# Another order for the first loads of a fused attention and feed-forward kernel: two tiles of x, projection weights, two tiles, then eleven weight blocks

## Chip, cores and metric

The kernel runs on one core of a Trainium2 chip. The metric is the device time of one execution in microseconds; lower is better.

## What is computed

The input x has shape (4, 512, 512): a batch of four, 512 tokens, 512 features. Cut to what matters:

```python
xn = layernorm(x)                                  # over the features, no weights
q, k, v = split(xn @ w_qkv)                        # 16 heads of 32
q, k = rope(rmsnorm(q, q_gamma)), rope(rmsnorm(k, k_gamma))
s = softmax(causal(q @ k.T / sqrt(32))) @ v @ w_out
W = lambda wq, scale: (wq - 128.0) * scale[:, None]  # int32 weights, 1408 hidden
g = silu((silu(xn @ W_gate.T) * (xn @ W_up.T)) @ W_down.T)
return x + s * g
```

All arrays are float32 but the three quantised weights, which are int32.

## The kernel before

The work is cut into 16 units, one for each batch `b` of four and each group `g` of four heads. A unit is a *hidden window* (`hidden_window`: the gate and up products of two or three blocks of 128 hidden columns, in `chunks[g]`) and an *attention window* (`attention_window`: scores, softmax and values of four token tiles `s[0]` to `s[3]`, with the down products `contract` and the projection and rotation of the next unit between them). Nothing plans this at run time: the pools are under a manual schedule, so each engine executes its instructions in the order in which the program writes them. What an engine waits for holds up all that is written after it on that engine. This applies to SyncE (SP) and its DMA queue too.

Ahead of the first unit stands `prologue`. It normalises the four tiles of batch 0, projects them for group 0, and starts the pipeline of the weights. Its parts, with the lines of the profile:

- `load_x` (L122) loads one tile of 128 tokens on SP. `Norm.stats` (L315, L316) takes mean and variance on VectorE, `Norm.roots` (L301, L302) the inverse root on GpSimd, `Norm.apply` (L323) scales the tile in place on VectorE, `Norm.turn` (L331, L334, L335) transposes it on TensorE and copies it on ScalarE twice, as `xnT` and as its rounded `xh`; `Norm.low` (L339) forms the rest `xl` on GpSimd.
- `Projection.product` (L353) multiplies one tile by the q, k and v columns of one group: four matmuls of fp32. `Projection.rotate` applies the norm of q and k and the rotary table: a square and a copy of v on ScalarE (L368, L369), three products and a sum on VectorE (L381, L384, L388), then four GpSimd instructions (L389, L301, L302, L391). `Projection.turn` (L401) transposes q and k into `qT` and `kT` at the third stop of the first hidden window.
- `prepare_table` (L193, L196) folds `q_gamma` and `k_gamma` (tile `gam`) into the rotary table `tab`.
- An int32 weight block goes through three stages. `load_weights` (L236) loads a block of 256 KB into a free room; `turn_weights` casts it on ScalarE (L245) and transposes it by DMA on SP (L247); `finish_weights` (L254) subtracts 128 on VectorE and writes the final weights. Blocks come in a fixed order: gate and up of hidden block 0 and 1 (g0, u0, g1, u1), four down blocks (d0 to d3), then g2, u2, g3, u3, g4 and so on. There are eleven rooms at the start, so that at most eleven blocks can be loaded before one is finished.
- `load_wqkv` (L147) loads the projection weights of group 0 ahead of the prologue in four pieces of 192 KB, and those of the other three groups at its end in four pieces of 576 KB. `sdown` is a broadcast row of 256 KB (L803).

Within the windows of batch 0, `weights()` keeps this pipeline going. At each call it finishes up to two blocks that were turned at least two calls ago, loads two more, and turns two that were loaded at least one call ago:

```python
for _ in range(n):
    if turning and now[0] - turning[0][0] >= 2:
        finish_weights()
load_weights(n)
for _ in range(n):
    if loaded and now[0] - loaded[0][0] >= 1:
        turn_weights()
```

The first hidden window calls it twice, after each of its two hidden blocks. So on ScalarE the casts of g2 and u2 are written between the SiLU of the first hidden block (L532) and that of the second, ahead of the copy of `qT` (L114); the casts of g3 and u3 are written ahead of the first exponentials (L447). On TensorE the order there is: gate and up of block 0 (L521), gate of block 1, the transposes of q and k (L401), up of block 1, the first scores (L419), the first down products (L549), scores, down products, the transposes of the first probabilities (L463), and the projection of the next unit.

Of the kernel before, what the change touches and what calls it, by code (L numbers as in the profile page):

```python
# [21 lines left out]
P = 128  # L22
# [3 lines left out]
NT = N // P  # L26
# [25 lines left out]
def interleaved(  # L52
# [27 lines left out]
    nc = tc.nc  # L80
# [19 lines left out]
    def work(name):  # L100
        return wk.tile([P, N], F32, tag="wk", name=name)
# [18 lines left out]
    def load_x(b, t):  # L120
        xt = xp.tile([P, D], F32, tag="x", name=f"x_{b}_{t}")
        nc.sync.dma_start(xt, xf[ts(b * NT + t, P), :])  # L122
        x_tiles[b, t] = xt
# [7 lines left out]

    ident = const.tile([P, P], F32, name="ident")
    make_identity(nc, ident)
    for t in range(NT):
        load_x(0, t)

    gam = work("gam")[:, 0 : 4 * HD].rearrange("p (a c d) -> p a c d", a=2, c=2)
    for i, g in enumerate((q_gamma, k_gamma)):
        nc.scalar.dma_start(gam[:, i, 0, :], g.partition_broadcast(P))
    tab = const.tile([P, NT, 2, 2, HD], F32, name="tab")  # L140
    nc.scalar.dma_start(tab, rope.rearrange("(t p) a c d -> p t a c d", p=P))

    wqkv = const.tile([P, NC, 3, NC, P], F32, name="wqkv")

    def load_wqkv(groups):
        for c in range(NC):
            nc.sync.dma_start(  # L147
                wqkv[:, c, :, groups, :],
                w_qkv[ts(c, P), :].rearrange("p (i g d) -> p i g d", i=3, g=NC)[:, :, groups, :],
            )  # L150

    load_wqkv(slice(0, 1))


    mask = const.tile([P, N], F32, name="mask")
# [18 lines left out]
    def load_scales():  # L174
        srow = work("srow")
        at = 0
        for s in (s_gate, s_up):
            n = s.shape[0] // P
            nc.sync.dma_start(srow[at : at + n, 0:P], s.rearrange("(c p) -> c p", p=P))
            at += n  # L180
        return srow, at
# [3 lines left out]
    def prepare_scales(srow, at):  # L185
        tp = bank_t("sps")
        nc.tensor.transpose(tp[:, 0:at], srow[0:at, 0:P], ident[0:at, 0:at])
        nc.vector.tensor_copy(scales, tp[:, 0:at])

    def prepare_table():  # L190

        for lo, hi in ((0, half), (half, 0)):
            nc.vector.tensor_copy(gam[:, :, 1, lo : lo + half], gam[:, :, 0, hi : hi + half])  # L193
        tab_f = tab.rearrange("p t a c d -> p t (a c d)")
        gam_f = gam.rearrange("p a c d -> p (a c d)")
        nc.vector.tensor_tensor(  # L196
            tab_f, tab_f, gam_f.unsqueeze(1).to_broadcast([P, NT, 4 * HD]), ALU.mult
        )
# [31 lines left out]
    def load_weights(n):  # L230
        for _ in range(n):
            if todo and rooms:
                src, k, dst, name = todo.pop(0)
                room = rooms.pop(0)
                raw = room[:, : k * P]
                nc.sync.dma_start(raw.bitcast(U32), src.bitcast(U32))  # L236
                loaded.append((now[0], room, raw, k, dst, name))

    def turn_weights():


        _, room, raw, k, dst, name = loaded.pop(0)
        halves_ = raw.bitcast(BF16)
        n = k * P
        nc.scalar.copy(halves_[:, :n], raw.bitcast(U32))  # L245
        turned = halves_[:, n:].rearrange("p (c r) -> p c r", r=P)
        nc.sync.dma_start(turned, halves_[:, :n], transpose=True)  # L247
        turning.append((now[0], room, turned, k, dst, name))

    def finish_weights():  # L250

        _, room, turned, k, dst, name = turning.pop(0)
        i = len(finished)
        nc.vector.tensor_scalar(  # L254
            dst,
            turned,
            -ZERO_POINT,
            None,
            ALU.add,
            ALU.max,  # L260
            accum_out=largest[:, i : i + 1],
        )
        if len(finished) >= NC:
            rooms.append(room)
        finished.add(name)
# [507 lines left out]

    def prologue():
        norm, fresh = Norm(0), Projection(0, 0)
        load_weights(4)
        scales_in = load_scales()
        load_weights(4)
        for t in range(NT):
            norm.stats(t)  # L780
            norm.roots(slice(t, t + 1))
            if t:
                norm.apply(t - 1)
                norm.turn(t - 1)
        norm.apply(NT - 1)
        norm.turn(NT - 1)
        prepare_table()
        for t in range(NT):
            norm.low(t)
        for _ in range(4):  # L790
            turn_weights()
        fresh.product(0)
        fresh.rotate(0)
        for _ in range(4):
            turn_weights()
        for t in range(1, NT):
            fresh.product(t)
            fresh.rotate(t)
            if t > 1:
                finish_weights()  # L800
                finish_weights()
        load_wqkv(slice(1, NC))
        nc.sync.dma_start(sdown, s_down.partition_broadcast(P))  # L803
        load_weights(3)
        now[0] += 1
        prepare_scales(*scales_in)
        return fresh

    fresh, last, norm = prologue(), None, None
    for u, (b, g) in enumerate(units):  # L810
        result = Result(b - 1) if g == 0 and b else None
        beside = [[], [], []]
        if g == NC - 2 and b + 1 < B:
            for t in range(NT):
                load_x(b + 1, t)
            norm = Norm(b + 1)
# [17 lines left out]
        fresh = Projection(*units[u + 1])  # L834
# [435 lines left out]
def attn_times_ffn(tc: tile.TileContext, *args: bass.AP):  # L1270

    nc = tc.nc
    with tc.tile_pool(name="flag", bufs=1) as flag:
        wide = flag.tile([1, 1], I32, name="wide")
        interleaved(tc, *args, wide=wide)
        over = nc.values_load(wide, min_val=0, max_val=1)
        with tc.If(over != 0):
            in_float32(tc, *args)
# [36 lines left out]
```

## Time and profile before

| what | value |
|---|---|
| time, median of 3 runs | 731.41 us |
| the three runs | 731.48, 731.41, 729.94 us |
| the profiled execution: its own time | 731.89 us |
| the profiled execution: span | 730.0 us |
| TensorE busy | 693.2 us, 95% |
| VectorE, ScalarE, GpSimd busy | 398.1, 372.1, 340.3 us |
| bytes moved by DMA | 31.18 MB, mean 43 GB/s |
| mean granted clock of TensorE | 0.993 |

The profile is of one execution. It starts some time after the launch and ends with the last instruction, so that its span is 1.9 us below the time of the same execution. Times inside it are counted from the span's start. A line such as `14.81 9.47 PE qkv L353 x26` in the chain of waits reads: from 14.81 us on, for 9.47 us, TensorE matmuls that write the tile `qkv` at line 353 held the chain, 26 of them. TensorE has two rows: PE for matmuls, PEld for the loads of the stationary operand; fp32 matmuls show as two records each.

### The profile page before, as it was taken

How to read it: one execution, taken by the hardware profiler on the slowest of the kernel's cores; microseconds unless marked ns; L12 is line 12 of the kernel's file. 1: busy time of each engine (PE TensorE's matmuls, PEld its weight loads, DVE VectorE, ACT ScalarE, POOL GpSimd, SP SyncE). 2: the span in 40 equal slices, each digit the busy share in tenths (PEclk: the TensorE clock that was granted, in tenths of full speed). 3: DMA queues.
4: the chain of work that ended last, by engine and by line, in shares of the span. 5: the costliest groups of instructions: out<-in, count | busy, mean ns of one | idle time of the engine just before them, and what ended most of it. 6: DMA issues, size and time to landing. Idle time of an engine off the chain costs nothing.

```text
span 730.0 us, 12109 instructions
## 1 busy us (share of the span) xinstructions
PE 693.2 (95%) x4386; PEld 460.3 (63%) x4386; DVE 398.1 (55%) x1168; ACT 372.1 (51%) x953; POOL 340.3 (47%) x387
## 2 busy tenths in 40 slices
PE   4979999999999999999999999999999999999995
PEld 2645757576565666768565576767656566676752
DVE  4547676655446255665635436475644535546463
ACT  4356765456644255555654255455664424555550
POOL 6715335346723535354753533545572452525422
PEclk9989999999999999999999999999999999999999
DMA  7645734000011200000001020000001100001001
GB/s 238 195 132 129 176 77 129 21 1 1 0 44 44 87 1 2 1 1 1 1 14 60 29 74 1 1 1 1 1 1 44 44 29 1 1 1 53 8 1 62
DMA packets 34735, 31.18 MB, mean 43 GB/s; under 512 B 19798, under 2 KB 24172, under 8 KB 34668
## 3 DMA queue, kind: packets, MB, share of 16 engines
q1 hardware_dynamic: 33708, 29.91, 14.2%
q8 instruction: 36, 0.59, 0.4%
q10 hardware_dynamic: 960, 0.43, 0.2%
q14 instruction: 31, 0.25, 0.1%
HBM read 21.80 MB, written 4.19 MB: 36 GB/s over the span
## 4 chain that ended last, share of the span: by engine, by line
PE 85%; DVE 5%; ACT 3%; POOL 2%; DMA 2%; issue 2%; SPq 1%; DVEq 0%; ACTq 0%
PE h L521 22%; PE qkv L353 20%; PE dn L549 12%; PE pt L463 9%; PE so L590 8%; PE sc L419 5%; PE pv L475 5%; PE qkt L401 2%; ACT pr L447 2%; DMA oT<-in_L_ffn_wq_up 1%; DVE acc L562 1%; PE xnt L331 1%; DMA x<-in_L_attn_x 1%; PE rt L499 1%; POOL ss L302 1%
## 5 line engine op out<-in xcount | busy, mean ns | idle before, releaser
L447 ACT ACTIVATE pr<-pr,least 128x128 f32<-128x128 f32 (+3 forms) x256 | 140.8, 551 | 111.8 <-DVE least L437 111.6
L353 PE MATMUL qkv<-wqkv,xnT 128*128 128x384 f32 x512 | 178.4, 493 | 3.3 <-ACT xnT L334 2.0
L389 POOL TENSOR_TENSOR qk<-qk,qs 128x256 f32<-128x256 f32 x64 | 46.7, 730 | 208.2 <-DVE qs L384 203.6
L353 PEld LDWEIGHTS qkv<-wqkv,xnT 128*128 128x128 f32 x512 | 93.5, 192 | 61.1 <-DVE least L437 4.9
L437 DVE CUSTOM_DVE_ANT_0 pr<-sc,mask 128x128 f32<-128x128 f32 (+3 forms) x256 | 111.6, 486 | 18.6 <-PE sc L419 16.6
L540 POOL TENSOR_TENSOR h<-sil,h 128x512 fp32r<-128x512 f32 x44 | 57.3, 1303 | 124.1 <-ACT h L539 124.1
L302 POOL TENSOR_TENSOR ss<-ss,minus_half 128x8 f32<-128x8 f32 x64 | 106.7, 1667 | 5.3
L549 PE MATMUL dn<-wdT,h 128*128 128x512 f32 x352 | 103.0, 425 | 4.3 <-DVE acc L562 1.8
L116 DVE COPY pT<-pt 128x512 f32<-128x512 f32 (+1 forms) x100 | 64.0, 642 | 56.0 <-PE pt L463 56.0
L463 PEld LDWEIGHTS pt<-ident,pr 128*128 128x128 f32 x640 | 73.5, 141 | 33.2 <-issue 24.1
L463 PE MATMUL pt<-ident,pr 128*128 128x128 f32 x640 | 87.6, 275 | 0.0
L549 PEld LDWEIGHTS dn<-wdT,h 128*128 128x128 f32 x352 | 62.7, 191 | 32.1 <-DVE acc L562 8.2
L538 DVE SCALAR_TENSOR_TENSOR sil<-h,scales,sil 128x512 f32<-128x512 f32 x44 | 33.0, 751 | 78.1 <-PE h L521 68.2
L381 DVE TENSOR_TENSOR qk<-qkv,tab 128x256 f32<-128x256 f32 x64 | 27.2, 425 | 86.8 <-ACT v L369 85.0
L521 PE MATMUL h<-xh,wgT 128*128 128x512 f32 x176 | 73.4, 417 | 0.0
L521 PE MATMUL h<-xh,wuT 128*128 128x512 f32 x176 | 72.2, 410 | 0.0
L521 PE MATMUL h<-xl,wgT 128*128 128x512 f32 x176 | 69.9, 397 | 1.8 <-POOL xl L339 1.8
L539 ACT CAST h<-sil 128x512 fp32r<-128x512 f32 x44 | 27.3, 620 | 86.6 <-DVE sil L538 86.6
L521 PE MATMUL h<-xl,wuT 128*128 128x512 f32 x176 | 69.6, 395 | 0.0
L368 ACT ACTIVATE sq<-qkv 128x256 f32<-128x256 f32 x64 | 24.6, 385 | 72.3 <-PE qkv L353 67.5
L419 PE MATMUL sc<-kT,qT 32*128 32x512 f32 (+3 forms) x512 | 54.2, 487 | 5.4 <-ACT qT L114 5.4
L590 PE MATMUL so<-wout,oT 128*128 128x512 f32 x128 | 59.1, 601 | 0.0
(87 smaller groups left out, 918.2 us busy)
## 6 DMA issues: line engine op xcount, KB each, us to landing
x<-in_L_attn_x SPq DMA_DIRECT2D x16, 256.0 KB, 4.0
out<-o SPq DMA_DIRECT2D x15, 256.0 KB, 2.0
xr<-in_L_attn_x SPq DMA_DIRECT2D x12, 256.0 KB, 2.7
wqkv<-in_L_attn_w_qkv SPq DMA_DIRECT2D x4, 576.0 KB, 5.0
wout<-in_L_ffn_wq_up SPq DMA_DIRECT2D x6, 256.0 KB, 2.8
wout<-in_L_ffn_wq_down SPq DMA_DIRECT2D x5, 256.0 KB, 3.9
wout<-in_L_ffn_wq_gate SPq DMA_DIRECT2D x5, 256.0 KB, 3.3
oT<-in_L_ffn_wq_gate SPq DMA_DIRECT2D x4, 256.0 KB, 5.8
```

The lines of the kernel that those rows point to most:

```text
L116: nc.vector.tensor_copy(dst, src)
L302: nc.gpsimd.tensor_tensor(dst, dst, minus_half[:, : dst.shape[-1]], ALU.pow)
L353: nc.tensor.matmul(bank.rearrange("p (i d) -> p i d", i=3), lhsT=xnT[:, c, ts(t, P)], rhs=wqkv[:, c, :, self.g, :], start=(c == 0), stop=( ...
L389: nc.gpsimd.tensor_tensor(qk, qk, qs, ALU.add)
L419: nc.tensor.matmul(bank[:, : self.keys], lhsT=qT[rows, ts(self.t, P)], rhs=kT[rows, : self.keys], start=True, stop=True,)
L437: nc.vector.tensor_tensor_reduce(out=pr, in0=self.banks[j][:, : self.keys], in1=mask[:, N - self.keys :], scale=float(HD), scalar=3.0e38, ...
L447: nc.scalar.activation(pr, pr, AF.Exp, bias=least, scale=-1.0, accum_out=self.sums[:, self.t, j : j + 1],)
L463: nc.tensor.transpose(tp[:, ts(i * (self.t + 1) + k, P)], self.probs[n * self.per + i][:, ts(k, P)], ident,)
L521: nc.tensor.matmul(bank, lhsT=w[:, c, ts(f, P)], rhs=a[:, c, :], start=(c == 0 and a is xh), stop=(c == NC - 1 and a is xl),)
L540: nc.gpsimd.tensor_tensor(to[:, 1, :], sil, to[:, 0, :].bitcast(F32), ALU.subtract)
L549: nc.tensor.matmul(bank, lhsT=h[:, i, a, ts(t, P)], rhs=wdT[:, f, :], start=(i == 0 and a == 0), stop=(f == fs[-1] and a == 1),)
L590: nc.tensor.matmul(self.banks[t], lhsT=oT[:, g, ts(t, P)], rhs=wout[:, g, :], start=(g == 0), stop=(g == NC - 1),)
```

## The change

The prologue's loads and its order are rewritten; the rest of the kernel is the same.

- The first two tiles of x are loaded ahead of the projection weights of group 0, the other two after them.
- `gam` and `tab` are loaded on SP, between the second and the third weight block, instead of on ScalarE's queue at the start.
- All eleven first weight blocks are loaded in the prologue's beginning. Three of them (g2, u2, g3) were loaded at its end, after the rest of the projection weights.
- A tile is scaled and transposed right after its own statistics, instead of after the statistics of the next tile, and the projection of tile t - 1 is written right after the transposes of tile t. Before, all four projections followed all transposes.
- Two weight blocks are turned after tile 3's copies, ahead of `prepare_table` and the first rotation; six more between the first and the second rotation (before: four ahead of the first rotation, four after it). Two blocks are finished before the second rotation and two before the fourth (before: two after the third rotation and two after the fourth).

```diff
     make_identity(nc, ident)
-    for t in range(NT):
-        load_x(0, t)
+    load_x(0, 0)
+    load_x(0, 1)
 
     gam = work("gam")[:, 0 : 4 * HD].rearrange("p (a c d) -> p a c d", a=2, c=2)
-    for i, g in enumerate((q_gamma, k_gamma)):
-        nc.scalar.dma_start(gam[:, i, 0, :], g.partition_broadcast(P))
     tab = const.tile([P, NT, 2, 2, HD], F32, name="tab")
-    nc.scalar.dma_start(tab, rope.rearrange("(t p) a c d -> p t a c d", p=P))
...
     load_wqkv(slice(0, 1))
+    load_x(0, 2)
+    load_x(0, 3)
...
         norm, fresh = Norm(0), Projection(0, 0)
-        load_weights(4)
+        load_weights(2)
+        for i, g in enumerate((q_gamma, k_gamma)):
+            nc.sync.dma_start(gam[:, i, 0, :], g.partition_broadcast(P))
+        nc.sync.dma_start(tab, rope.rearrange("(t p) a c d -> p t a c d", p=P))
+        load_weights(2)
         scales_in = load_scales()
-        load_weights(4)
+        load_weights(7)
         for t in range(NT):
             norm.stats(t)
             norm.roots(slice(t, t + 1))
+            norm.apply(t)
+            norm.turn(t)
             if t:
-                norm.apply(t - 1)
-                norm.turn(t - 1)
-        norm.apply(NT - 1)
-        norm.turn(NT - 1)
-        prepare_table()
+                fresh.product(t - 1)
+        turn_weights()
+        turn_weights()
         for t in range(NT):
             norm.low(t)
-        for _ in range(4):
+        fresh.product(NT - 1)
+        prepare_table()
+        fresh.rotate(0)
+        for _ in range(6):
             turn_weights()
-        fresh.product(0)
-        fresh.rotate(0)
-        for _ in range(4):
-            turn_weights()
-        for t in range(1, NT):
-            fresh.product(t)
-            fresh.rotate(t)
-            if t > 1:
-                finish_weights()
-                finish_weights()
+        finish_weights()
+        finish_weights()
+        fresh.rotate(1)
+        fresh.rotate(2)
+        finish_weights()
+        finish_weights()
+        fresh.rotate(3)
         load_wqkv(slice(1, NC))
         nc.sync.dma_start(sdown, s_down.partition_broadcast(P))
-        load_weights(3)
         now[0] += 1
```

## The prediction

> **What bounds the kernel now.** I read the page's slices first, for where TensorE is not full. Each digit is a fortieth of the span, 18.25 us.
>
> ```profile
> PE   4979999999999999999999999999999999999995
> PEclk9989999999999999999999999999999999999999
> DMA  7645734000011200000001020000001100001001
> ```
>
> TensorE is full from the fourth slice on; the change touches only the first three. From about 47.6 us on TensorE hardly pauses (windows of 0.5 us from 47.5 to 54.5 are busy throughout), so what the change is worth is how far it moves the first attention transposes (L463, weights loaded at 47.65). I call this **the mark**. A shift of the mark passes to the end, and the mark needs the first four exponentials (L447, 44.80 to 46.44).
>
> Next, the chain that ended last, cut to 0 to 48 us (start, duration, what):
>
> ```profile
> 0.72 5.55 DMA x<-in_L_attn_x
> ...
> 11.47 1.10 PE xnt L331 x4
> ...
> 13.72 1.09 PE xnt L331 x4
> 14.81 9.47 PE qkv L353 x26
> ...
> 29.65 0.65 SPq L803
> 30.30 0.05 issue
> 30.35 0.74 SPq L236
> 31.09 0.04 issue
> 31.14 8.64 DMA oT<-in_L_ffn_wq_up
> ```
>
> x is waited for until 6.27, TensorE turns four tiles and projects them, and SP, after eight transposes, issues the rest of the projection weights (26.99 on), `sdown`, and the ninth to eleventh weight blocks (g2, u2, g3). Those land behind 2.6 MB. The waits of 30 to 48 us show who stands still (waiter, releaser, us in total, times, longest):
>
> ```profile
> ACT oT L245 <- DMA oT<-in_L_ffn_wq_gate: 6.1, 1, 6.1
> PE sc L419 <- ACT qT L114: 5.4, 1, 5.4
> ```
>
> ScalarE stands before the cast of g2 until 39.14; behind it in its order lie a SiLU and the copy of qT, so TensorE idles from 36.12 to 41.54.
>
> Last, TensorE's weight loads at the first projection:
>
> ```profile
> 15.88 0.34 PEld L353 LDWEIGHTS qkv<-wqkv,xnT 128*128 128x128 f32 x1 [0.30 <-issue]
> 16.52 0.34 PEld L353 LDWEIGHTS qkv<-wqkv,xnT 128*128 128x128 f32 x1 [0.30 <-issue]
> 17.02 8.58 PEld L353 LDWEIGHTS qkv<-wqkv,xnT 128*128 128x128 f32 x27 [0.17 <-issue]
> ```
>
> Up to 17.0 a load takes 0.34 us and comes every 0.64; after that 0.19 us every 0.32. TensorE starts at half rate, though PEclk says 1.00 there. After the idle stretch it falls again: PEclk is 0.50 from 40.7 to 47.5.
>
> **What the Trainium skill says.** "TensorE: Matmul & The Clock Gate", section "What's actually happening": the clock is halved by default and after an idle window, and freed after a busy one, in free-running windows of 3413 ns. The trace agrees: 40.7 to 47.5 is two such windows, and full rate comes at 17.0, after dense work from 13.7. "DMA: Bandwidth & Descriptors", section "Issuing engines are not separate DMA queues": SP's and ScalarE's transfers share the same engines, and a second issuer saves only sequencer time. The trace shows both waiting together at the start: ScalarE's 16 KB `gam` takes about as long to land (5.3 us) as the first x (5.55). "Perfetto Trace Analysis", section "DMA Instruction — HWDGE (DVE, Sync)": the profiled duration of a DMA instruction leaves out the data movement. Here u2 shows 0.65 us of issue and lands after 8.64.
>
> **The change, part by part.** Times are in the profiled execution's clock.
>
> *Loads.* ScalarE loses three issues (0.40, 0.45, 0.46 us); its engine was idle until 9.98, worth nothing. SP issues x0, x1, four `wqkv` pieces, x2, x3 in about 4 x 0.44 + 4 x 0.64 = 4.3 us without the 2.5 us wait that SP had before its second `wqkv` piece. x2 and x3 fall behind 0.79 MB: at some 300 KB/us they land near 10, before VectorE reaches them. `gam` and `tab` are wanted only at 15. x0 no longer shares its start with them: landing T is bounded by 6.3 (nothing gained) and 3.4 (the 2.7 us of a later single load). DMA was only half busy until 4 us, so sharing explains little; I take T = 5.7.
>
> *Each tile at once.* VectorE now waits for GpSimd's root before scaling. The first tile shows that serial length: 6.29 to 8.77 = 2.48 us. Tiles 0 and 1 are scaled at T + 5.0 = 10.7; four transposes, 1.1 us; the first projection starts at 11.8 instead of 14.60. But that start is cold. With dense work from 10.7, full rate comes between 13.7 and 17.2; I take 15.2. The first projection (5.15 us cold, 2.58 warm) then ends at 11.8 + 3.4 + 0.9 = 16.1. Tile 2's transposes (0.55 warm), projection 1 (2.58), tile 3's transposes (0.55): tile 3 is turned at 19.8, before at 14.81. All four projections end at 25.0, before at 26.0: one microsecond won.
>
> *What hangs on tile 3.* ScalarE's order puts the casts after the copies of tile 3: 1.1 + 0.63 us, so the first DMA transpose goes at 21.45 instead of 16.46. The eight take SP 10.5 us (16.46 to 26.94), so the rest of the projection weights goes at 31.95 instead of 26.99, **5.0 us late**.
>
> *The three early blocks.* g2, u2, g3 now land by 19, before the transposes, whose long stretch leaves DMA half idle; cost nothing, and their casts wait for nothing. The 6.1 us stall goes. What is late next is u3, issued after `sdown`: before, it landed at 41.16, 14.2 us after the first of the rest; less three blocks at 0.67 us gives 12.2, so 31.95 + 12.2 = 44.15. ScalarE's cast of u3 stands ahead of the exponentials: 0.62 for the cast, 1.3 table load, 1.64 for four exponentials: **47.7**. Before, they were done at 46.44 and TensorE, at half rate, reached the mark at 47.65.
>
> *The other path to the mark.* Rotation 0 enters GpSimd at 23.5 (copies to 20.9, two casts 1.15, Square and copy 0.54, VectorE 0.86) instead of 19.98. Six casts (3.15 us) lie before rotation 1 on ScalarE; it enters at 27.2. Three passes of 3.36: qk complete at 37.3, before at 33.42. TensorE idles from 31.7 (second gate block done, three transposes) to 37.3, 5.6 us, where it had 5.4: it most likely falls to half rate again. Then five transposes (1.1) and the last up block (3.7 at half rate) end at 42.1; VectorE 0.75 and two more weight blocks 1.36 give 44.3, two `dn` groups with the scores between them put the mark at 47.4. At full rate it would be 45.5, and u3 decides.
>
> **Sum:** the later of 47.7 and 47.4 against 47.65: +0.05 us, that is nothing. The profiled execution took 731.89 around a span of 730.0; the runs shown have a median of 731.41, 0.48 below it, and I forecast from the median: 731.4.
>
> **The rivals.**
> *Faster: the start is quicker than I put it.* For it: x0 takes 5.5 us where later loads take 2.7, and the ScalarE queue is cleared. With T = 4.5 and full rate at 14.7 tile 3 is turned 1.5 us earlier, u3 decides at 46.2; if `wqkv` alone also drains some 0.4 us faster, 45.8: -1.85 us, 729.6. Against it: the half-rate start hits a whole projection now.
> *Slower: u3 decides from a late start.* With x0 at 6.3 and full rate at 17.2, tile 3 is turned at 21.4 (+1.6); every step from there to u3 is serial on ScalarE, SP and the DMA queue, so exponentials end at 49.3. With 0.4 us more for u3: +2 us, 733.4. It decides from a tile 3 turned after 21.2. For it: eight transposes and 2.6 MB stand between tile 3 and u3 with no slack. Against it: `wqkv` has the DMA engines to itself.
> *The moves do nothing.* If x and weights land as before and the stall is just exchanged, the result is also zero.
> A run-to-run part is in all three: the windows are free-running, and 731.48, 731.41, 729.94 look like two with and one without the half-rate stretch at 41 us.
>
> **How the numbers follow.** About 0.2%, 1.46 us, is what a measurement here can tell from no change. Zero is the likeliest (0.41), its own range 730.0 to 732.9; slower 0.32, as unlisted waits mostly add; faster 0.27. T (-2.3, +0.6), the time of full rate (half of -1.5, +2.0) and u3's landing (1 us either way) do not all add; the range that keeps 8 in 10 is 729.3 to 733.6.
>
> **What would show it.** After: first statistics at 5.7; first projection at 11.8; tile 3 turned near 19.8; first DMA transpose near 21.5; rest of the weights near 32; no wait for g2; a wait of ScalarE for u3 (an `L245` cast after a DMA of `wq_up`) until 44; GpSimd's last product near 37.3. Wrong if ScalarE meets u3 already landed, if the transposes go before 20, or if TensorE's idle stretch is gone: then faster. If the stretch lies elsewhere or another load is waited for, the sum was right by luck at best.

## The result, and the profile after

The change makes the kernel faster by a little: a median of 728.42 us over 7 runs (727.67 to 729.12) against 730.68 us (729.94 to 731.48) for the kernel before on the same chip. The ratio is 0.9968, with a 95% interval of 0.9956 to 0.9979, so 2.3 us are gained. The forecast was 731.4, in a range of 729.3 to 733.6: the result lies 0.9 us below the range. It was a forecast of no change, from the median of 731.41 over three runs; 0.7 of the 3.0 us by which it missed is that starting point, and 2.3 us are the change itself. The profiled execution took 728.74 around a span of 726.9; before they were 731.89 and 730.0. What follows explains these 3.1 us between the two profiled executions, which are somewhat more than the 2.3 us between the medians.

Line numbers in the new file are one lower in most places (L353 is L352, L521 is L520, L463 is L462). First the slices of the page, each now 18.17 us (726.9 / 40):

```profile
PE   5799999999999999999999999999999999999995
PEclk9889999999999999999999999999999999999998
DMA  8675634000011200000001020000001100001001
```

The first slice of TensorE rose from 4 to 5 and the second fell from 9 to 7: TensorE starts earlier, and its idle stretch has moved from the third slice (before 7, now 9) into the second. The stretch itself is no longer than before: 5.5 us, from 28.3 to 33.8 and broken by one transpose, where it was 5.4. From the fourth slice on nothing has changed, as the forecast supposed. The clock is below full in the second and third slice, where before only the third was.

The chain that ended last in the kernel after, cut to 0 to 46 us (start, duration, what):

```profile
0.72 2.82 DMA x<-in_L_attn_x
...
8.48 1.12 PE xnt L330 x4
9.60 3.49 PE qkv L352 x8
...
33.10 0.62 POOL qk L390
33.77 1.33 PE qkt L400 x5
35.10 3.43 PE h L520 x8
...
45.00 0.72 PE pt L462 x4
```

The wait for x is 2.82 us where it was 5.55. The step from SP through a late weight block to ScalarE (8.64 us, L236 and L245) is gone from the chain; GpSimd's rotation of q and k (L390) has taken its place. The waits of 30 to 48 us say the same (waiter, releaser, us in total, times, longest):

```profile
PEld qkt L400 <- POOL qk L390: 5.6, 2, 3.2
ACT h L538 <- DVE sil L537: 5.4, 2, 4.5
```

No engine waits for g2, and ScalarE waits for no DMA at all in this stretch. TensorE's weight loads at the first projection, then at the mark:

```profile
10.68 0.34 PEld L352 LDWEIGHTS qkv<-wqkv,xnT 128*128 128x128 f32 x1 [0.30 <-issue]
11.32 1.16 PEld L352 LDWEIGHTS qkv<-wqkv,xnT 128*128 128x128 f32 x4 [0.30 <-DMA tab<-in_rope]
...
44.38 0.22 PEld L462 LDWEIGHTS pt<-ident,pr 128*128 128x128 f32 x1
```

Full rate comes at 11.3 instead of 17.0. The mark is the last of these lines; before, it was this one:

```profile
47.65 0.59 PEld L463 LDWEIGHTS pt<-ident,pr 128*128 128x128 f32 x4
```

It comes 3.3 us earlier, which is the 3.1 us of the span but for 0.2.

SP's own queue shows the serial part behind tile 3 (transposes, then the rest of the projection weights, then u3; start, duration of the issue):

```profile
18.21 5.25 SPq L246 DMA_TRANSPOSE room<-room  x4
...
28.74 2.63 SPq L144 DMA_DIRECT2D wqkv<-in_L_attn_w_qkv  x4
...
32.15 0.35 SPq L235 DMA_DIRECT2D wout<-in_L_ffn_wq_up  x1
```

The forecast had 21.45 for the first and 31.95 for the third line; both came 3.2 us earlier. u3 lands 7.9 us after its issue, at 40.05, and ScalarE casts it at 40.46 without having waited for it. The transposes before 20 and u3 already landed are two of the signs which the forecast named as "then faster".

### The profile page after: what moved, and what is told of

It is laid out like the page before. It is cut to its first block, busy times and chain, and to the rows that moved or that the text cites. A ratio compares the mean times of both kernels' runs of the same rounds, so it can differ in the third digit from the quotient of the medians.

```text
span 726.9 us, 12113 instructions
## 1 busy us (share of the span) xinstructions
PE 693.5 (95%) x4386; PEld 460.1 (63%) x4386; DVE 398.4 (55%) x1168; ACT 371.8 (51%) x953; POOL 340.1 (47%) x387
## 4 chain that ended last, share of the span: by engine, by line
PE 85%; DVE 5%; POOL 4%; ACT 3%; issue 1%; DMA 1%; DVEq 0%; ACTq 0%
PE h L520 22%; PE qkv L352 20%; PE dn L548 12%; PE pt L462 9%; PE so L589 8%; PE sc L418 5%; PE pv L474 5%; PE qkt L400 2%; ACT pr L446 2%; POOL ss L301 1%; DVE acc L561 1%; PE xnt L330 1%; PE rt L498 1%; POOL qk L388 1%; POOL h L539 1%
## 5 line engine op out<-in xcount | busy, mean ns | idle before, releaser
L352 PE MATMUL qkv<-wqkv,xnT 128*128 128x384 f32 x512 | 178.6, 492 | 3.3 <-ACT xnT L333 2.0
L352 PEld LDWEIGHTS qkv<-wqkv,xnT 128*128 128x128 f32 x512 | 93.1, 191 | 60.6 <-DVE least L436 4.8
L462 PEld LDWEIGHTS pt<-ident,pr 128*128 128x128 f32 x640 | 73.9, 141 | 33.4 <-issue 24.4
L462 PE MATMUL pt<-ident,pr 128*128 128x128 f32 x640 | 87.9, 276 | 0.0
L520 PE MATMUL h<-xh,wgT 128*128 128x512 f32 x176 | 73.4, 417 | 0.2 <-DVE wgT L253 0.2
L520 PE MATMUL h<-xh,wuT 128*128 128x512 f32 x176 | 73.1, 416 | 0.0
L520 PE MATMUL h<-xl,wgT 128*128 128x512 f32 x176 | 69.8, 397 | 1.8 <-POOL xl L338 1.8
L520 PE MATMUL h<-xl,wuT 128*128 128x512 f32 x176 | 70.4, 400 | 0.0
```

Source lines behind the costliest of these rows:

```text
L352: nc.tensor.matmul(bank.rearrange("p (i d) -> p i d", i=3), lhsT=xnT[:, c, ts(t, P)], rhs=wqkv[:, c, :, self.g, :], start=(c == 0), stop=( ...
L462: nc.tensor.transpose(tp[:, ts(i * (self.t + 1) + k, P)], self.probs[n * self.per + i][:, ts(k, P)], ident,)
L520: nc.tensor.matmul(bank, lhsT=w[:, c, ts(f, P)], rhs=a[:, c, :], start=(c == 0 and a is xh), stop=(c == NC - 1 and a is xl),)
```

## The experiments

Names that begin with a are the kernel after with one edit, those with b the kernel before with one. Differences are of medians, against the kernel before on the same chip in the same rounds. The kernel before itself had medians of 730.68 to 731.29 in the different sets of rounds, so a difference between two versions of different sets is good to about 0.6 us. Q is the theory that `gam` and `tab` on ScalarE's queue hold up the first tile of x; E that the three early blocks give the gain; O that the new order of the tiles costs some of it.

**The parts, one at a time.** b_gamtab_sp moves only the loads of `gam` and `tab`:

```diff
-    for i, g in enumerate((q_gamma, k_gamma)):
-        nc.scalar.dma_start(gam[:, i, 0, :], g.partition_broadcast(P))
...
-    nc.scalar.dma_start(tab, rope.rearrange("(t p) a c d -> p t a c d", p=P))
...
-        load_weights(4)
+        load_weights(2)
+        for i, g in enumerate((q_gamma, k_gamma)):
+            nc.sync.dma_start(gam[:, i, 0, :], g.partition_broadcast(P))
+        nc.sync.dma_start(tab, rope.rearrange("(t p) a c d -> p t a c d", p=P))
+        load_weights(2)
```

> The kernel before, with one thing changed: gam and tab are no longer loaded on ScalarE's queue at the start but on SP between the second and third weight block. If ScalarE's transfers held up the first x (theory Q), x0 lands near 3.6 us instead of 6.3, everything up to the late g2 block moves 2.7 us forward with it (the rest of the projection weights is issued near 24.3, g2 lands near 36.4) and the time falls by 2 to 2.7 us, to about 728.3: the whole gain of the change. If x0 landed early because only two tiles of x stand ahead of the projection weights (theory S), x0 stays near 6 us and the time near 730.7. If the eleven early blocks are the gain (theory E), nothing changes either.

Measured: 728.94 against 731.29, ratio 0.9970 (0.9959 to 0.9982), 2.3 us gained. The first statistics start at 3.34 instead of 6.29, 3.0 us earlier, the transposes at 13.71 and the rest of the weights at 24.26, 2.7 us earlier. The wait for g2 stays, at 5.9 us. So the start is worth 2.3 us by itself, with nothing else changed.

b_early11 loads only the three blocks early:

```diff
-        load_weights(4)
+        load_weights(7)
...
-        load_weights(3)
         now[0] += 1
```

> The kernel before, with one thing changed: g2, u2 and g3 are loaded with the other eight blocks. Theory E (the early blocks bring the gain, by taking ScalarE's stall away): with the compute order of before, qk is complete at 33.4 us, the up block of hidden block 1 ends at 36.1 and the scores follow at once; u3 lands 12.2 us after the rest of the projection weights is issued at 27.0, so at 39.2, and the mark comes near 42.8 instead of 47.65: about 726. Theory Q: the blocks only exchange one late block for the next, and the time is within 1 us of before, 730 to 731.

Measured: 724.99 against 731.29, ratio 0.9925 (0.9912 to 0.9937), 6.3 us gained, x0 still at 5.69. The wait for g2 is gone, TensorE has no stretch at half rate, and the mark is at 40.31. This one part of the change gains nearly three times what the whole change does, and more than was expected of it.

b_gamtab_early11 has both edits, with the old order and x in one piece.

> The kernel before with both: gam and tab on SP and all eleven blocks early, but x in one piece ahead of the projection weights and the tiles in the old order. If both parts work and add (theories Q and E), x0 at 3.6, qk near 31, u3 near 36.6 and the mark near 40.5: about 724, faster than the changed kernel, and the new order of the tiles costs 4 us. If the new order of the tiles is itself worth something (theory T), the time stays above 728.4.

Measured: 724.22 over 4 runs, ratio 0.9902 (0.9888 to 0.9917), 7.1 us gained, **well ahead of the kernel before and the kernel after**. It has the lowest median here, but its interval overlaps with that of b_early11, so that it beats that version isn't shown. The two gains (2.3 and 6.3) would make 8.6; the 1.5 us that are missing are about as much as the intervals leave open. Its profiled execution, at 725.43 slower than its median, shows two things that cost: full rate only at 17.4, and a stretch at half rate from 37.9 to 41.3.

b_neworder takes the kernel before and changes only the loop over the tiles to the new order (scale, transpose and project in turn, casts after tile 3, rotations as in the change).

> The kernel before with its own loads, and only the new order of tiles, casts and rotations. By the prediction's sum tile 3 is turned 4 to 5 us later, the eight transposes and the rest of the weights follow, and g2, which ScalarE waits for, lands near 43.5 instead of 39.1: 734.5 to 736. If the new order is a gain that the changed kernel shows (theory T), 728 to 730.

Measured: 737.05 against 730.96, ratio 1.0088 (1.0075 to 1.0101), 6.1 us lost. The rest of the weights goes at 32.36, 5.4 us late, ScalarE waits 8.1 us for g2, and the mark is at 52.5. The loss is 1 us above the range expected of it. The delay is the one that the forecast had worked out for "What hangs on tile 3" (5.0 us).

**Undoing one part of the change.** a_late3 puts the three blocks back to the prologue's end (the diff of b_early11 reversed).

> The changed kernel with g2, u2 and g3 loaded at the prologue's end again. If the early blocks pay for the later transposes (theory E beside Q), ScalarE stands before g2 as in the kernel before, but later: the rest of the projection weights goes at 28.7, g2 lands 12.1 us after it, at 40.9, the mark moves from 44.7 to about 49.4 and the time rises by 4 to 5 us, to about 733. If the early blocks matter little in this order (theory Q alone), under 1 us: 728 to 729.5.

Measured: 735.56 against 730.96, ratio 1.0060 (1.0047 to 1.0073), so the early blocks are worth about 7 us in the kernel after, where 4 to 5 had been expected. The waits show what comes back:

```profile
ACT oT L244 <- DMA oT<-in_L_ffn_wq_gate: 8.6, 1, 8.6
```

a_gamtab_act puts the loads of `gam` and `tab` back on ScalarE's queue at the start (the diff of b_gamtab_sp reversed).

> The changed kernel, with gam and tab put back on ScalarE's queue at the start. Theory Q: x0 lands near 6.3 us again, tile 3 is turned 2 to 2.7 us later and the time rises to 730.5 to 731.2, as the sum of the prediction had it. Theory S: x0 stays at 3.6 us and the time at 728.4.

Measured: 731.58 against 731.29, ratio 1.0007 (0.9999 to 1.0015). With this one part undone the gain is gone; the time lies 0.4 us above the range expected. x0 is at 5.44 (forecast 5.7), the first projection at 11.26 (11.8), tile 3 turned at 19.56 (19.8), the transposes at 21.21 (21.45), the rest of the weights at 31.76 (31.95). What follows is not as forecast. u3 lands near 42.9 instead of 44.15, and ScalarE casts it without having waited for it:

```profile
42.82 0.62 ACT L541 CAST h<-sil 128x512 fp32r<-128x512 f32 x1 [4.96 <-DVE sil L540]
43.35 0.61 ACT L247 CAST oT<-oT 128x512 bf16<-128x512 uint32 x1
43.87 0.61 ACT L247 CAST wout<-wout 128x512 bf16<-128x512 uint32 x1
```

The mark is at 48.67 in this profiled execution (732.88, 1.3 us above the median), behind GpSimd's rotation and a stretch at half rate from 36.0 to 49.6. So the median, 731.58, is next to the forecast of 731.4, but not by the forecast's path: that it comes so near is in part luck.

a_oldorder keeps all loads of the kernel after and goes back to the old order of the tiles, casts and rotations.

> The changed kernel's loads in full (two tiles of x, projection weights, two tiles, eleven blocks, gam and tab on SP), with the prologue's old order of tiles, casts and rotations. If the new order of the tiles is what costs against b_gamtab_early11 (theory O), about 725; x2, landing 3 us later than in that kernel, costs up to 1 us of it: 724.5 to 725.7. If it is the split of x that costs (theory X), about 728.4, as in the changed kernel.

Measured: 726.46 against 730.96, ratio 0.9940 (0.9927 to 0.9953): the new order costs about 2 us against this. Neither expectation is met. This version is over 2 us behind b_gamtab_early11, where up to 1 us had been expected, though it differs only in that x2 and x3 come after the projection weights. In the old order all projections wait for tile 3, and here VectorE waited 4.05 us for x2, until 9.96.

a_x4 tests the same in the new order: all four tiles of x ahead of the projection weights.

```diff
-    load_x(0, 0)
-    load_x(0, 1)
+    for t in range(NT):
+        load_x(0, t)
...
-    load_x(0, 2)
-    load_x(0, 3)
```

> The changed kernel with all four tiles of x ahead of the projection weights. In the old order of tiles the split of x costs 2 us (724.2 against 726.5), as VectorE waits 4 us for x2 and every projection is written after tile 3. In the new order TensorE is at work on the first projection while x2 lands: VectorE's wait of 1.3 us goes, but tile 2 is not turned before that projection ends at 12.9, and the projection weights land 1.5 us later. So within 0.7 us of the changed kernel: 727.7 to 729.1. If the split costs 2 us here too, about 726.4; if it pays in this order, 729.5 or more.

Measured: 728.22 against 731.18, ratio 0.9957 (0.9944 to 0.9969), as the kernel after. In the new order splitting x makes no measurable difference. a_x4 and b_gamtab_early11 have the same loads in the same places, so they give the price of the order alone: about 4 us. The rest of the weights goes at 28.62 against 25.18, and qk is complete at 33.6 against 32.5. TensorE shows what becomes of its early start. Here is the table by stretches of 2 us for b_gamtab_early11 (stretch, length, then busy time of PE, PEld, VectorE, ScalarE, GpSimd, then PEclk, DMA share and GB/s):

```profile
28.00:30.00 2.00, 2.00 (x11) 1.59 (x10) 0.68 (x3) 1.24 (x1) 1.92 (x4) 1.00 1.05 391
30.00:32.00 2.00, 1.59 (x9) 1.08 (x7) 1.22 (x2) 1.17 (x3) 1.84 (x3) 1.00 1.03 350
```

and for the kernel after:

```profile
28.00:30.00 2.00, 0.26 (x3) 0.02 (x1) 0.67 (x4) 1.25 (x1) 1.90 (x2) 1.00 0.35 68
30.00:32.00 2.00, 0.33 (x1) 0.14 (x1) 1.23 (x2) 1.17 (x3) 1.92 (x4) 0.95 0.77 227
```

GpSimd is full in both (1.84 to 1.92 of 2 us): its passes of 3.36 us set when qk is complete, and in the new order they start later (20.07 in the kernel after, 19.94 in a_x4, 19.09 in b_gamtab_early11). ScalarE's square for the first rotation, first in the kernel after, then in b_gamtab_early11:

```profile
18.59 0.40 ACT L367 ACTIVATE sq<-qkv 128x256 f32<-128x256 f32 x1
```

```profile
17.61 0.38 ACT L365 ACTIVATE sq<-qkv 128x256 f32<-128x256 f32 x1 [1.94 <-PE qkv L350]
```

In the kernel after, the first projection was complete at 13.1, but ScalarE's order puts this square behind the copies of tile 3 and two casts. In the old order the first projection is complete only at 17.6, and its square follows at once. The new order ends the projections at 21.6 and the work after them at 28.3; then TensorE waits until 33.77 and is at half rate from 31.8 to 38.6. In the old order it is at work until qk is nearly there and waits for it 1.0 us.

**Is the half rate what costs?** a_filler keeps TensorE busy in the gap with 20 matmuls whose product nothing reads, ahead of the transposes of q and k:

```diff
     def turn(self):
 
+        if self.b == 0 and self.g == 0:
+            warm = ps_d.tile([P, N], F32, tag="dn", name="warm")
+            for i in range(20):
+                nc.tensor.matmul(
+                    warm, lhsT=wgT[:, i % NC, ts(0, P)], rhs=xh[:, i % NC, :], start=True, stop=True
+                )
```

> The changed kernel with twenty further matmuls (128x128 by 128x512, 4.7 us at full rate) on TensorE between the gate of hidden block 1 and the transposes of q, into a PSUM bank that nobody reads: they lie in the idle stretch of 28.3 to 33.8 us and hold no data up. If the half rate after that stretch is a cost of its own (theory H), the up block of hidden block 1 takes 1.9 us instead of 3.4, the mark comes 1.5 to 2.5 us earlier and the time falls to 726 to 727. If the mark hangs on u3 or on VectorE instead, the time stays within 0.5 us of 728.4.

Measured: 729.05 over 18 runs (727.77 to 731.92), ratio 0.9981 (0.9971 to 0.9990): no gain over the kernel after. The profiled execution is one of the quicker ones, at 728.49. In it TensorE kept full rate until 39.6 and the last up block took 2.1 us instead of 3.43, but ScalarE then met the next wait:

```profile
ACT wout L244 <- DMA wout<-in_L_ffn_wq_up: 2.8, 1, 2.8
```

That is u3, cast at 41.58 instead of 40.46, since in this run the second group of four transposes took 6.25 us instead of 5.14. The mark was at 44.06. So in these two profiles two paths end within half a microsecond of each other, GpSimd and the half rate on one, the transposes and u3 on the other, and taking the half rate away bought nothing. What it would have bought had the transposes taken 5.14 us isn't shown.

**What holds up x0?** a_gam_act and a_tab_act each put only one of the two loads back on ScalarE's queue; one profiled execution of each.

> The changed kernel with only gam (two broadcasts of 16 KB in 128-byte rows) back on ScalarE's queue at the start; tab stays on SP. If the first x waits because of gam, x0 lands near 5.5 us; if tab's 256 KB is what it shares its start with, x0 stays near 3.6 us.

> The changed kernel with only tab (256 KB) back on ScalarE's queue at the start; gam stays on SP. If tab's bytes hold x0 up, x0 lands near 5 us or later; if gam does, x0 stays near 3.6 us. If either transfer on the second queue does it, both kernels show x0 near 5.5.

Measured: x0 is at 4.98 with `gam` alone (732.53 us) and at 3.71 with `tab` alone (731.16 us). It is `gam`, for most of the delay: with both on that queue x0 was at 5.44. The time of a_tab_act doesn't follow its x0: its first projection took 4.86 us, full rate coming late; a single run can't settle more. The table by stretches shows it too. Two stretches of the kernel before, with the same columns as above:

```profile
2.00:3.00 1.00, 0.00 (x0) 0.00 (x0) 0.00 (x0) 0.88 (x1) 0.50 (x2) 1.00 0.11 38
3.00:4.00 1.00, 0.00 (x0) 0.00 (x0) 0.00 (x0) 0.40 (x1) 0.00 (x0) 1.00 0.38 131
```

of the kernel after:

```profile
2.00:3.00 1.00, 0.00 (x0) 0.00 (x0) 0.00 (x0) 0.01 (x1) 0.50 (x2) 1.00 0.75 270
3.00:4.00 1.00, 0.00 (x0) 0.00 (x0) 0.43 (x1) 0.00 (x0) 0.00 (x0) 1.00 0.88 296
```

of a_gam_act:

```profile
2.00:3.00 1.00, 0.00 (x0) 0.00 (x0) 0.00 (x0) 0.94 (x1) 0.50 (x2) 1.00 0.39 87
```

and of a_tab_act:

```profile
2.00:3.00 1.00, 0.00 (x0) 0.00 (x0) 0.00 (x0) 0.50 (x1) 0.50 (x2) 1.00 0.80 250
```

The last two columns decide: with `gam` in ScalarE's queue all DMA together moves 38 or 87 GB/s in the third microsecond, without it 250 or 270. With `tab` alone in that queue nothing is lost there, so it isn't the queue as such.

a_gamtab_act_late asks whether it is ScalarE's queue or the moment: it issues both there, after tile 0's copies.

> The changed kernel with gam and tab on ScalarE's queue, but written after the copies of tile 0, so issued near 8.3 us. If only their sharing of the start with x0 costs (theory Q), x0 lands at 3.6 us and the time is that of the changed kernel, 728 to 729. If ScalarE's queue itself costs, 730.5 or more, as with both at the start (731.6).

Measured: 729.99 over 17 runs, ratio 0.9986 (0.9979 to 0.9994), between the two expectations. x0 is at 3.51, so the moment matters. Why it is still slower than the kernel after, ScalarE's instructions show:

```profile
12.65 0.38 ACTq L786 DMA_DIRECT2D gam<-in_L_attn_q_gamma  x1
...
14.37 0.58 ACT L333 COPY xnT<-xnt 128x512 f32<-128x512 f32 x1 [6.10 <-DMA srow<-in_L_ffn_s_up]
```

Its issue of `gam`, next in order from the end of tile 0's copies at 8.26, waited until 12.65, and with the two issues after it kept tile 1's copies back until 14.37. That is a wait of its own, so this run doesn't say what the queue alone would cost.

## Why the prediction was wrong, point by point

**The step that failed is the landing of x0.** The forecast bounded T by 6.3 and 3.4 and took 5.7, because "DMA was only half busy until 4 us, so sharing explains little". Measured: 3.57, near the lower bound. The reason was read the wrong way round. The half-busy DMA was what `gam` did to it, not a sign that there was room: all DMA together, x0 in it, moves 270 GB/s where `gam` isn't under way. The Trainium skill, "DMA: Bandwidth & Descriptors", section "Issuing engines are not separate DMA queues", says that transfers of all issuers run on the same 16 engines and interleave; I had used it for what a second issuer saves, and not for what its small transfer costs the large one beside it. a_gamtab_act is the counter-test: with T back at 5.44 the gain is gone, and every step up to the rest of the weights lies within 0.6 us of the forecast.

**A second term was off by 1.8 us in this run:** full rate at T + 9.5, forecast, came at T + 7.7 = 11.3. The bounds given were T + 8.0 and T + 11.5, so it lies just outside, and it moves from run to run: in a_late3, with the same start, it came near 13.1, T + 9.6. Tile 3 was turned at 16.57 instead of 19.8: 2.1 of these 3.2 us are T, and most of the rest is this term (1.8 us at half rate, so 0.9).

**A third step failed behind these: u3 was to decide.** The forecast had u3 12.2 us after the first of the rest of the weights, and ScalarE waiting for it until 44. In the kernel after it came after 11.3 us, in a_gamtab_act after 11.2, and ScalarE waited for it in neither. GpSimd's path, forecast only 0.3 us shorter, set the mark instead: 44.38, 10.7 us after qk was complete, where the forecast had 10.1.

**What held.** The serial 2.48 us of a tile (3.57 to 6.05). The eight transposes in 10.5 us. The early blocks ending the wait for g2. GpSimd's three passes after rotation 0, with qk complete 3.6 us ahead of forecast, as all upstream of it. An idle stretch of 5.5 us (forecast 5.6) and the fall to half rate after it. And the balance of two paths near the mark, u3's and GpSimd's, which a_filler shows in its one profile.

**The rivals.** The faster one had the right cause, a quicker start, and 729.6 for T = 4.5; with T at 3.57 and earlier full rate it passes below. It was given 0.27, too little, since the one argument against a small T was the misread one. The slower one (T of 6.3) is out. "The moves do nothing" would have been wrong on the mechanism even if the time had come out at zero: a near-zero sum is what a_gamtab_act shows, and it is made of the early blocks, worth 6.3 to 7.1 us, and an order that costs 2 to 6, by what stands beside it.

What stays open: why two broadcasts of 16 KB slow a load of 256 KB this much. The page named above has, under "Why small descriptors are slow (HBM only)", a fixed cost for each packet, 27% at 256 bytes; the rows of `gam` are 128 bytes, and 270 against 87 GB/s is far more than that. No run here goes further. Nor was it tried why the split of x costs over 2 us in the old order beyond the wait for x2 seen in one profile.

## What to carry to other kernels

Before taking the first load's landing as given, look at what else is in flight in the same microseconds: a low DMA share there can be the damage and not the room. Measure the parts of a change one by one; here one part of it gains 6.3 us and the whole 2.3, because another part, the order of the tiles, gives back what the first wins. Starting the busiest engine earlier is worth nothing if the engine that feeds its next step doesn't start earlier too: the time comes back as one long gap, and a gap can cost clock.

## What the runs showed of the hardware

- Two broadcasts of 16 KB issued on ScalarE's queue beside the first 256 KB load on SP's delay that load: statistics at 4.98 with `gam`, 3.71 with `tab`, 5.4 to 6.3 with both, 3.3 to 3.6 with neither.
- TensorE's clock also fell after stretches in which it wasn't idle. The Trainium skill, "TensorE: Matmul & The Clock Gate", section "What's actually happening", has half rate after an idle window of 3413 ns. The steps of PEclk here agree with that length: in the kernel after it falls near 31.8, rises near 38.6, falls near 42.0 and rises near 45.4. But the window before the second fall was 66% busy. Same columns as above:

```profile
38.58:41.99 3.41, 2.26 (x16) 1.32 (x19) 2.82 (x14) 2.56 (x4) 1.28 (x1) 0.99 1.42 235
41.99:45.40 3.41, 3.41 (x15) 2.27 (x16) 2.15 (x9) 3.40 (x15) 0.00 (x0) 0.51 0.96 182
```

  In a_filler a window with 2.11 of 3.41 us busy, up to 39.6, was followed by half rate as well. The busy share alone doesn't decide it, though. In the kernel before, counting windows back from the fall near 40.8, one that was 64% busy was followed by full rate, and only the idle one after it by half rate:

```profile
33.94:37.35 3.41, 2.17 (x11) 1.46 (x9) 0.69 (x1) 0.00 (x0) 0.73 (x1) 1.00 1.03 319
37.35:40.77 3.42, 0.00 (x0) 0.00 (x0) 0.00 (x0) 1.58 (x3) 0.00 (x0) 1.00 0.83 304
```

  The busy windows that half rate followed held matmuls of the scores (`sc`, 32*128 in the trace), whose stationary operand has 32 rows; the one of the kernel before held only matmuls with 128 rows. Whether that is the difference, no run here shows.
- The row PEclk says 1.00 at the kernel's start, while the spacing of weight loads (0.64 us, later 0.32) shows half rate until 11.3 (the kernel after) to 20.3 us (a_oldorder), depending on the version and the run.
- A DMA issue on a compute engine can itself wait, here 4.4 us, and then everything behind it on that engine waits too.
